# A six-block decoder: value projections moved into the router's gap, key rotation by a DVE shuffle, and a reordered start of attention

## The chip, the core and the metric

The kernel runs on one core of one Trainium2 chip. Its engines work side by side: PE multiplies matrices, DVE and POOL do elementwise work and reductions, ACT does functions and copies, SP only issues transfers. Every engine takes its own instructions in order and waits for the others through semaphores. The metric is the device time of one execution in microseconds, as the median of several runs.

## The reference, cut to what matters

A decoder of six blocks, each with a residual sum and a layer norm behind it. The input `x` is 4 sequences of 512 rows and 256 columns, the context 4 sequences of 1601 rows and 256 columns, all in float32.

```python
x = _layernorm(x + _L0_attn_ref(...))    # a recurrent layer (TTT)
x = _layernorm(x + _L0_xattn_ref(...))   # one-headed attention over the context
x = _layernorm(x + _L0_ffn_ref(...))     # 8 experts, the best 2 for each row
x = _layernorm(x + _L1_attn_ref(...))    # causal self-attention, 16 heads of 16
x = _layernorm(x + _L1_xattn_ref(...))   # cross-attention, 16 heads of 16, rotary
x = _layernorm(x + _L1_ffn_ref(...))     # dense feed-forward
```

The change concerns the third to the fifth block. In the fifth, queries and keys are projected, rotated and then used; the values are projected only:

```python
def apply_rope(x, cos, sin):
    x2 = jnp.stack([-x[..., 1::2], x[..., 0::2]], axis=-1).reshape(x.shape)
    return x * cos + x2 * sin
Q = (query @ Wq.T + bq)...; K = (key @ Wk.T + bk)...; V = (value @ Wv.T + bv)...
Q = apply_rope(Q, cos_q, sin_q); K = apply_rope(K, cos_k, sin_k)
```

`query` is `x`, `key` and `value` are the context. So keys and values of this block depend on nothing that the earlier blocks compute.

## The kernel before, in words

**Stages in time.** The recurrent layer runs to about 250 us, the one-headed attention and the router to 485 us, the experts from 521 to 1020 us, the fourth and fifth block from there to about 2335 us, and the last feed-forward behind them. Sequences (`b`), row tiles of 128 (`t`) and key tiles of 128 (`k`, 13 of them for the 1601 context rows, `NKT`) are the loop indices; the 16 heads form 4 groups (`g`, `NG`).

**Order of the work.** In most stages the program's own order is kept on every engine. What stands outside such a stretch (the loads of the attention weights into the pool `plw`, and `blocks_left`, which works out which expert blocks are left) is put in place by a planner that simulates a list schedule by readiness. Tiles of a pool that takes over the memory of an earlier pool wait until all of that pool's readers are through. `plw` and `p3` follow `p2in` and `p2` in this way.

**The router's gap (second block's end).** In pool `p2`, each step (b, t) makes scores, transposes the weights and sums the context rows with them (`weighted`). Behind the last `weighted` of a sequence follows the generator `closing(b)`: layer norm, `xT[b]` by transposes, then `route` (router logits, exponent, the best two, their ranks by a matmul) and `scatter(b)`, which writes the rows of `x` to the experts' list `xs` in DRAM by eight indirect transfers of POOL. `tail()` runs one step of such a generator. For the last sequence nothing else is left to do:

```python
        while tails:
            tail()
        ordered.close()
        scatter(B - 1, lambda inst: unordered("xs", inst))
```

Then the experts load their blocks of `xs` (`begin`, tile `xb`, L835) on SP, behind the loads of the attention weights (L79 to L85). The two biggest tiles of the stage's inputs are `fs`, the additive mask (128 x 4 x 1601), and `ctxa`, context rows of a sequence. Both are in `p2in` and read for the last time by the last scores and by the last `weighted`.

**The experts.** 23 blocks of 256 rows. `first_half` makes the gated hidden layer, `second_half` the second product, the norm, and `gamma` and `beta` on POOL (L909, L910); the result goes to `ys` in DRAM by an SP transfer. At each block one step of the generator `attention_first` runs, which prepares the next stage: context 0 into tiles (`qt`, `ks`), tables for the rotation, `vself`, `vals`, and at its end two small products for the output bias (`bo_x`, `bob`). It has 24 steps for 22 calls; what is left runs behind the last block.

**The gap behind the experts (L1010 on).** `combined(0)` gathers the experts' rows of sequence 0 by POOL's indirect transfers, adds them to `x` on DVE (`added`, L1091), normalizes, and transposes (`turned`). Only then can the self-attention of sequence 0 be projected: `self_rows(b, c)` makes key and query rows, which go through DRAM (`ksd`, `qd`) into the tiles of the head groups; `self_values(b)` makes its values. Meanwhile the kernel works on the contexts. `context(b, keys, values)` gives a list of small work items for a context: an item `key` (L1187) projects 512 keys of half the heads, evicts them by ACT into a `raw` tile (four buffers), rotates them and sends them to `kcd`; an item `value` (L1196) projects 128 rows by four matmuls of 256 columns and copies them by ACT into `vals[b % 2]`. Its context comes by SP transfers of 512 columns (`chunk`, two buffers). `rotated` (L1145 to L1157) makes the pair-swapped copy `swp` (two buffers) by two SP transfers between partitions of SBUF, then multiplies and adds on DVE for context 0 and on POOL for all others, queries included.

**The attention units.** 16 self units and then 16 cross units (b, g). A unit first takes maxima of its scores (`slot1`, DVE: L1272 in cross units, L1274 in self units), then for each key tile makes the scores again (L1315), exponents on ACT (L1329) and the weighted sums (L1342). Two lists carry other work into the units, one item at a time: `extras` (PE work: projections, keys and values of the next sequences) and `quiet`. `starts[i]` holds transfers that are issued as unit i begins. Keys and values of context 1 are made around the self units; those of contexts 2 and 3 in the cross units of sequences 0 to 2:

```python
        later = [
            context(2, range(4), ()) + context(3, range(2), ()),
            context(3, range(2, 4), ()) + context(2, (), range(4)),
            context(3, (), range(4)),
        ]
```

Of the kernel before, what the change touches and what calls it, by code (L numbers as in the profile page):

```python
# [9 lines left out]
F32 = mybir.dt.float32  # L10
# [3 lines left out]
ALU = mybir.AluOpType  # L14
# [20 lines left out]
def kn_of(kt):  # L35
    return P if kt < NKT - 1 else KLAST
# [3 lines left out]
def decoder(ctx: ExitStack, tc: tile.TileContext, a: dict, out: bass.AP):  # L40
    nc = tc.nc
# [16 lines left out]
    def bank():  # L58
        return psum["B"].tile([P, 512], F32, tag="bank", name="bank")
# [15 lines left out]
    def weight(pool, name):  # L75

        src = a[name]
        t = pool.tile([P, 2, src.shape[1]], F32, tag=name, name=name)
        nc.sync.dma_start(t, src.rearrange("(c p) n -> p c n", p=P))  # L79
        return t  # L80
# [117 lines left out]
    def mm(ps, terms):  # L198

        n = len(terms)  # L200
        for i, (l, r) in enumerate(terms):
            nc.tensor.matmul(ps, l, r, start=(i == 0), stop=(i == n - 1))  # L202
# [3 lines left out]
    p2in = ph2in.enter_context(tc.tile_pool(name="p2in", bufs=1))  # L206


    with (
# [15 lines left out]
        ps = wide()  # L225
# [4 lines left out]
        ps = bank()  # L230
# [7 lines left out]
        fs = p2in.tile([P, NT, S2], F32, tag="fs", name="fs")  # L238
# [7 lines left out]
        KHALF = (NKT + 1) // 2  # L246
# [358 lines left out]
        return wrow, xrow  # L605


    with tc.tile_pool(name="p2", bufs=2) as p2, ExitStack() as ordered:


# [131 lines left out]
        scored(*steps[0])  # L742
        tails = []

        def tail():
            if tails and next(tails[0], tails) is tails:
                tails.pop(0)

        for i in range(len(steps) + 1):
            if i + 1 < len(steps):  # L750
                b, t = steps[i + 1]
                scored(b, t)
                if t == NT - 1:
                    more_columns(b + 2)
                    if b + 1 < B:
                        queries(b + 1)
            tail()
            if i < len(steps):
                turned(*steps[i])
            tail()  # L760
            if i > 0:
                b, t = steps[i - 1]
                weighted(b, t)
                if t == NT - 1:
                    if b + 1 < B:
                        ctxns[b + 1] = load_ctx(b + 1)
                    tails.append(closing(b))
            tail()
        while tails:
            tail()  # L770
        ordered.close()
        scatter(B - 1, lambda inst: unordered("xs", inst))
        wrow, xrow = blocks_left()
# [5 lines left out]


    QS = 1.0 / math.sqrt(HD)
    VW = HD + 1
    p4a = late_a.enter_context(tc.tile_pool(name="p4a", bufs=1))
    mrow = tc.dram_tile((4 * B, S2), F32, name="mrow")
    live = p4a.tile([P, 4 * B], F32, tag="live", name="live")
# [35 lines left out]
    with tc.tile_pool(name="p3", bufs=2) as p3, ExitStack() as ordered:  # L821
# [70 lines left out]
        def second_half(i, wo, xb, g):  # L892
            ps = bank()
            pv = ps.rearrange("p (h d) -> p h d", d=D)
            for h in range(2):
                blk = slice(h * P, (h + 1) * P)
                mm(pv[:, h, :], [(g[:, f, blk], wo[:, f * D : (f + 1) * D]) for f in range(NF)])
            r = p3.tile([P, 2, D], F32, tag="rb", name="rb")
            nc.vector.tensor_tensor(r, pv, xb, ALU.add)  # L899
            mv = moments(r, 2)  # L900
            rs = rstd_of(mv, eps12, 2)
            for h in range(2):
                nc.vector.tensor_scalar(
                    r[:, h, :], r[:, h, :], mv[:, h, 0:1], rs[:, h : h + 1], ALU.subtract, ALU.mult
                )
            gam, bet = (
                wo[:, None, (NF + k) * D : (NF + k + 1) * D].to_broadcast([P, 2, D]) for k in (1, 2)
            )
            nc.gpsimd.tensor_tensor(r, r, gam, ALU.mult)  # L909
            nc.gpsimd.tensor_tensor(r, r, bet, ALU.add)  # L910
            nc.sync.dma_start(ys[i * BLK : (i + 1) * BLK, :].rearrange("(h p) d -> p h d", p=P), r)

        def attention_first():
# [5 lines left out]
            ready["later"] = p4a.tile([P, 2 * P], BF16, tag="later", name="later")  # L919
            yield  # L920
            nc.gpsimd.tensor_copy(ready["later"], later)
            yield
            qt, ks = ready["qt"], ready["ks"] = [group_tiles(p4a, n, S) for n in ("qt", "ks")]

            at = qt + ks
# [24 lines left out]
            for i in range(2 * NT):  # L950
                t = p4a.tile([P, 4, 32], F32, tag=f"ng{i}", name=f"ng{i}")
                nc.gpsimd.memset(t, 0.0)
                ngs.append(t)
            yield
            ready["vself"] = [values_tile(p4a, f"vs{i}", NT) for i in range(2)]
            yield
            ready["vals"] = [values_tile(p4a, "v0", NKT)]
            yield

# [68 lines left out]
    with ExitStack() as s4:  # L1028
# [107 lines left out]
        def self_values(b):  # L1136


            def item(k):
                ps = one()[:, :D]  # L1140
                mm(ps, [(xT[b][:, c, k * P : (k + 1) * P], W["qkvV"][:, c, :]) for c in range(2)])
                dst = vself[b % 2][:, k, : NH * VW].rearrange("p (h r) -> p h r", r=VW)
                nc.scalar.copy(dst[:, :, :HD], ps.rearrange("p (h r) -> p h r", r=HD))

            return [lambda k=k: item(k) for k in range(NT)]  # L1145

        def rotated(raw, n, ks, eng, tables=None):

            cos, sin = tables or (cosT[:, ks], sinT[:, ks])
            swp = p4.tile([P, S + 1], F32, tag="swp", name="swp")[:, :S]  # L1150
            pairs = raw.rearrange("(a two) n -> a two n", two=2)
            into = swp.rearrange("(a two) n -> a two n", two=2)
            for i in range(2):
                nc.sync.dma_start(into[:, i, :n], pairs[:, 1 - i, :n])
            eng.tensor_tensor(raw[:, :n], raw[:, :n], cos[:, :n], ALU.mult)  # L1155
            eng.tensor_tensor(swp[:, :n], swp[:, :n], sin[:, :n], ALU.mult)
            eng.tensor_tensor(raw[:, :n], raw[:, :n], swp[:, :n], ALU.add)  # L1157
# [3 lines left out]
        def flush(n):  # L1161
            while len(going) > n:
                going.pop(0)()
# [436 lines left out]
            f()  # L1600
        for f in first_sums:
            f()
        cosT = const(p4c, "c_cos", [P, S2], nc.sync)
        sinT = const(p4c, "c_sin", [P, S2], nc.sync)
        for f in context(0, (), range(4), here=qt + kself):
            f()

        keys0 = context(0, range(4), (), here=qt + kself)
        (k0_, q0_), rows0 = self_rows(0, 0)
        (k1_, q1_), rows1 = self_rows(0, 1)  # L1610
        for f in keys0[0:2] + keys0[4:6] + values1[:6] + add + values1[6:] + turn:
            f()
        for f in (k0_, q0_, rows0, *keys0[2:4], *keys0[6:8], *self_values(0), k1_, q1_, rows1):
            f()
        flush(0)
        for i, (n0, n1) in enumerate(((0, 4), (4, 6), (6, 7), (7, 8))):
            extras[i] = keys1[n0:n1] + extras[i]
        later = [
            context(2, range(4), ()) + context(3, range(2), ()),
            context(3, range(2, 4), ()) + context(2, (), range(4)),  # L1620
            context(3, (), range(4)),
        ]
        for b, work in enumerate(later):
            for g in range(NG):
                n = -(-len(work) // (NG - g))
# [233 lines left out]
```

## Time and profile before

| quantity | value |
|---|---|
| median of 3 runs | 2454.46 us (2454.04 to 2455.28) |
| the profiled execution | 2460.01 us, its span 2458.2 us |
| mean granted PE clock in it | 0.964 |
| PE busy | 2349.0 us (96%) |
| DVE busy | 1187.0 us (48%) |
| ACT busy | 1074.2 us (44%) |
| POOL busy | 425.0 us (17%) |

By stage, from the busy time of the engines in stretches of the span:

| stretch, us | PE busy | DVE | ACT | POOL | clock |
|---|---|---|---|---|---|
| 252 to 486, one-headed attention | 231.0 | 89.4 | 47.5 | 17.6 | 0.99 |
| 486 to 521, router's gap | 9.9 | 13.3 | 3.0 | 13.5 | 0.53 |
| 521 to 1020, experts | 494.1 | 135.5 | 236.4 | 161.0 | 0.99 |
| 1020 to 1148, gap and first maxima | 105.5 | 56.8 | 37.5 | 48.2 | 0.81 |
| 1148 to 1520, self units | 362.4 | 236.2 | 179.7 | 69.9 | 0.95 |
| 1520 to 2335, cross units | 814.5 | 527.6 | 499.8 | 86.5 | 1.00 |

How to read it: all times are of one profiled execution and are counted from its first instruction. "Busy" leaves out the issuing of transfers. The clock is the share of full speed that PE was granted in the stretch; at half the clock a matmul takes longer and still counts as busy. Where a row of an answer shows an instruction, it gives the start, the length, the engine, the line of the kernel, the operation, and the tiles that it writes and reads ("out<-in"); brackets hold the idle time of the engine before it and what ended it.

### The profile page before, as it was taken

The page shows a single profiled execution, that of the slowest core. Times are in us where ns is not written, and L with a number is a line of the kernel's source. Part 1 is how long each engine was busy: PE and PEld are TensorE (multiplying, and loading weights), DVE is VectorE, ACT ScalarE, POOL GpSimd, SP SyncE. Part 2 cuts the span into 40 slices and gives each one's busy share as a digit, 9 for nine tenths or more (in the row PEclk, how much of TensorE's full clock was granted, in tenths as well). Part 3 has the DMA queues.
Part 4 walks back from the last instruction along what each step waited for, and adds up shares of the span by engine and source line. Part 5 has one row for each costly group of instructions (what it writes and reads, how often), then busy time and mean ns, then how long its engine had stood idle before and what let it go on. Part 6 is the DMA issues. An engine that isn't in the chain of part 4 may idle for free.

```text
span 2458.2 us, 34942 instructions
## 1 busy us (share of the span) xinstructions
PE 2349.0 (96%) x13928; PEld 1331.3 (54%) x13928; DVE 1187.0 (48%) x2772; ACT 1074.2 (44%) x1996; POOL 425.0 (17%) x431
## 2 busy tenths in 40 slices
PE   7998999959999999969999999999999999999998
PEld 4767677748888888743333334333333333333256
DVE  1333334422222222336666667666666666677334
ACT  1111222114455544324555553655566565556730
POOL 1010001121134444323330000222110010000000
PEclk9999999969999999978999998999999999999999
DMA  8300211234767555442211220122210110110100
GB/s 319 135 1 23 102 54 44 73 135 149 263 251 273 212 190 197 145 122 81 83 44 30 71 75 5 49 73 62 66 54 20 44 40 16 32 36 16 33 9 26
DMA packets 82513, 224.50 MB, mean 91 GB/s; under 512 B 14120, under 2 KB 37934, under 8 KB 73262
## 3 DMA queue, kind: packets, MB, share of 16 engines
q1 hardware_dynamic: 68190, 141.70, 17.1%
q0 software_dynamic: 10992, 65.54, 7.3%
q10 hardware_dynamic: 3168, 15.03, 1.8%
q8 instruction: 110, 1.80, 0.3%
q14 instruction: 53, 0.43, 0.1%
HBM read 171.53 MB, written 53.21 MB: 91 GB/s over the span
## 4 chain that ended last, share of the span: by engine, by line
PE 51%; ACT 1%; DVE 1%; issue 0%; DVEq 0%; ACTq 0%
PE s L1315 23%; PE one L202 12%; PE po L1342 11%; PE s L202 2%; PE s L1325 1%; PE one L1300 1%; PE one L1363 1%; ACT x L171 0%; ACT ex L1329 0%; DVE one L1274 0%; PE one L1384 0%; PE one L1405 0%; PE one L1482 0%; DVE pm L1272 0%; DVE st L156 0%
## 5 line engine op out<-in xcount | busy, mean ns | idle before, releaser
L1329 ACT ACTIVATE ex<-s 128x512 f32<-128x512 f32 (+1 forms) x1062 | 578.1, 594 | 480.5 <-PE s L1315 237.4
L1272 DVE TENSOR_REDUCE pm<-one 128x1 f32<-128x512 f32 x768 | 494.2, 686 | 203.7 <-PE s L1315 147.7
L1315 PE MATMUL s<-q,kc 32*128 32x512 f32 x1612 | 522.9, 640 | 0.2 <-ACT ex L1329 0.2
L202 PE MATMUL one<-kc,qt 32*128 32x512 f32 (+1 forms) x2048 | 483.6, 563 | 0.3 <-DVE pm L1272 0.3
L1315 PEld LDWEIGHTS s<-q,kc 32*128 32x128 f32 x1612 | 161.6, 179 | 210.2 <-issue 175.2
L1342 PE MATMUL po<-ex,v 128*32 128x256 f32 (+3 forms) x2472 | 245.8, 466 | 0.3 <-ACT ot L1355 0.3
L1274 DVE CUSTOM_DVE_ANT_0 one<-one,c_diagq 128x512 f32<-128x512 f32 x256 | 172.0, 716 | 89.2 <-PE one L202 78.3
L1315 PE MATMUL s<-q,ks 32*128 32x512 f32 x512 | 182.2, 660 | 4.9 <-ACT ex L1329 4.9
L1342 PEld LDWEIGHTS po<-ex,v 128*32 128x32 f32 (+1 forms) x2472 | 49.9, 108 | 233.0 <-issue 227.0
L886 DVE TENSOR_TENSOR g<-g,sg 128x1024 f32<-128x1024 f32 x46 | 57.3, 1246 | 238.3 <-ACT sg L883 238.3
L202 PE MATMUL wide<-xbT,eWi 128*128 128x256 f32 x736 | 168.4, 388 | 4.0 <-DVE xbT L858 4.0
L202 PEld LDWEIGHTS one<-kc,qt 32*128 32x128 f32 x2048 | 163.9, 188 | 11.7 <-DVE pm L1272 7.7
L202 PE MATMUL bank<-eWo,g 128*128 128x256 f32 x736 | 162.8, 379 | 0.5 <-DVE rb L899 0.5
L202 PE MATMUL wide<-xbT,eWg 128*128 128x256 f32 x736 | 162.9, 379 | 0.1
L202 PEld LDWEIGHTS wide<-xbT,eWi 128*128 128x128 f32 x736 | 143.6, 195 | 25.1 <-issue 3.4
L1155 POOL TENSOR_TENSOR raw<-raw,c_cos 128x512 f32<-128x512 f32 (+1 forms) x32 | 35.0, 1093 | 696.2 <-DMA swp<-raw 616.5
L202 PE MATMUL one<-ks,qt 32*128 32x512 f32 x512 | 153.4, 668 | 1.1 <-ACT raw L1126 1.1
L202 PEld LDWEIGHTS wide<-xbT,eWg 128*128 128x128 f32 x736 | 139.8, 190 | 19.5 <-ACT g L883 0.5
L202 PEld LDWEIGHTS bank<-eWo,g 128*128 128x128 f32 x736 | 138.1, 190 | 18.5 <-DVE rb L899 0.6
L883 ACT ACTIVATE g<-wide,eWi 128x256 f32<-128x256 f32 x184 | 71.9, 477 | 69.8 <-PE wide L202 67.0
L1315 PEld LDWEIGHTS s<-q,ks 32*128 32x128 f32 x512 | 54.1, 188 | 83.1 <-issue 61.9
L202 PE MATMUL wide<-ctxT,q 128*128 128x512 f32 (+1 forms) x256 | 91.3, 510 | 0.8 <-DVE q L649 0.8
(310 smaller groups left out, 2969.7 us busy)
## 6 DMA issues: line engine op xcount, KB each, us to landing
xs<-zero SPq DMA_DIRECT2D x32, 512.0 KB
kc<-kcd SPq DMA_DIRECT2D x16, 800.5 KB
eWo<-in_eWo SPq DMA_DIRECT2D x8, 1408.0 KB
cx<-in_ctxT SPq DMA_DIRECT2D x18, 512.0 KB
eWi<-in_eWi SPq DMA_DIRECT2D x8, 1028.0 KB
eWg<-in_eWg SPq DMA_DIRECT2D x8, 1028.0 KB
swp<-raw SPq DMA_DIRECT2D x64, 128.0 KB
qt<-qd SPq DMA_DIRECT2D x32, 256.0 KB
```

The lines of the kernel that those rows point to most:

```text
L202: nc.tensor.matmul(ps, l, r, start=(i == 0), stop=(i == n - 1))
L883: nc.scalar.activation(dst[:, k, :], pv[:, k, :], func, bias=bias)
L886: nc.vector.tensor_tensor(part, part, dst, ALU.mult)
L1155: eng.tensor_tensor(raw[:, :n], raw[:, :n], cos[:, :n], ALU.mult)
L1272: nc.vector.tensor_reduce(pm[:, t, j, c : c + 1], ps, AX.X, ALU.max)
L1274: nc.vector.tensor_tensor_reduce(out=ps, in0=ps, in1=diagq[:, 384 - t * P : 896 - t * P], scale=1.0, scalar=LOWEST, op0=ALU.add, op1=ALU.m ...
L1300: nc.tensor.transpose(pt[:, t * P : (t + 1) * P], ng.rearrange("p j r -> p (j r)"), ident)
L1315: nc.tensor.matmul(ps[:kn], kt[rows, k * P : k * P + kn], q2[rows, :], start=True, stop=cross)
L1325: nc.tensor.matmul(ps[:, k * P : (k + 1) * P], later_[:, :P], later_[:, P:], start=False, stop=True)
L1329: nc.scalar.activation(ex[:kn, h, :], ps[:kn], AF.Exp)
L1342: nc.tensor.matmul(state["po"][j * 32 : j * 32 + 32, q0:q1], (vals if cross else vself)[b % 2][:kn, k, c0 : c0 + 32], ex[:kn, j % 2, q0:q1 ...
L1363: nc.tensor.transpose(pt[:, t * P : (t + 1) * P], ot[:, t * P : (t + 1) * P], ident)
```

## The change

1. **Values of contexts 2 and 3** (26 items of four matmuls and one ACT copy) are made in the `while tails` loop, two behind each `tail()`, and the rest behind it. They are written into new tiles in the places of `fs` and `ctxa`, whose fixed columns (zeros and ones) POOL writes by memsets, and stored to new DRAM tensors `vd[2]` and `vd[3]` by SP. One SP transfer for each loads `vals[b % 2]` as the second cross unit of the sequence before begins (`starts[index[b - 1, 1, True]]`). Their items go from `later`, and with them the context chunks loaded for them.
2. **The pair swap** in `rotated` is one `stream_shuffle` on DVE in place of two SP transfers, for all 40 rotations (8 of context 0, 24 of contexts 1 to 3, 8 of queries). The arithmetic stays where it was.
3. **`gamma` and `beta`** of the last expert block go to DVE.
4. **Three `yield`s** of `attention_first` are taken out, which leaves 21 steps.
5. **The order behind the experts**: all values of context 1 and the addition of the experts' rows come ahead of the second pair of keys; the values of the first self-attention come ahead of the other two pairs; the full cosine and sine tables are loaded behind this work instead of ahead of it; the second half of the first self-attention's projections (`k1_`, `q1_`, `rows1`) moves into the first unit's `extras`.

```diff
+        xaV = weight(p2, "xaV")
+        values, places = [], {}
+        def value(b, k):
+            if not places:
+                big = p2in.tile([P, NT * S2], F32, tag="fs", name="v23")
+                rest = p2in.tile([P, KHALF * D], F32, tag="ctxa", name="v2")
...
+                for b_ in (2, 3):
+                    nc.gpsimd.memset(places[b_, NKT - 1], 0.0)
...
+            kn = kn_of(k)
+            ps = bank()[:, :D]
+            mm(ps[:kn], [(ctxTs[b][:, c, k * P : k * P + kn], xaV[:, c, :]) for c in range(2)])
+            dst = places[b, k][:kn, : NH * VW].rearrange("p (h r) -> p h r", r=VW)
+            nc.scalar.copy(dst[:, :, :HD], ps[:kn].rearrange("p (h r) -> p h r", r=HD))
+            if b == 2 and k == NKT - 1:
+                nc.sync.dma_start(vd[2][:, : 9 * VROW], big_of(2, 0, 9))
+                nc.sync.dma_start(vd[2][:, 9 * VROW :], big_of(2, 9, NKT))
+            if b == 3 and k == NKT - 1:
+                nc.sync.dma_start(vd[3], big_of(3, 0, NKT))
...
+        values = [lambda b=b, k=k: value(b, k) for b in (2, 3) for k in range(NKT)]
         while tails:
             tail()
+            for f in values[:2]:
+                f()
+            values = values[2:]
+        for f in values:
+            f()
         ordered.close()
         scatter(B - 1, lambda inst: unordered("xs", inst))
...
-            nc.gpsimd.tensor_tensor(r, r, gam, ALU.mult)
-            nc.gpsimd.tensor_tensor(r, r, bet, ALU.add)
+            eng = nc.vector if i == E + NDYN - 1 else nc.gpsimd
+            eng.tensor_tensor(r, r, gam, ALU.mult)
+            eng.tensor_tensor(r, r, bet, ALU.add)
...
-            pairs = raw.rearrange("(a two) n -> a two n", two=2)
-            into = swp.rearrange("(a two) n -> a two n", two=2)
-            for i in range(2):
-                nc.sync.dma_start(into[:, i, :n], pairs[:, 1 - i, :n])
+            nc.vector.stream_shuffle(swp[:, :n], raw[:, :n], [i ^ 1 for i in range(32)])
...
-        cosT = const(p4c, "c_cos", [P, S2], nc.sync)
-        sinT = const(p4c, "c_sin", [P, S2], nc.sync)
...
-        for f in keys0[0:2] + keys0[4:6] + values1[:6] + add + values1[6:] + turn:
+        for f in keys0[0:2] + values1 + add + keys0[4:6] + turn:
             f()
-        for f in (k0_, q0_, rows0, *keys0[2:4], *keys0[6:8], *self_values(0), k1_, q1_, rows1):
+        for f in (k0_, q0_, rows0, *self_values(0), *keys0[2:4], *keys0[6:8]):
             f()
+        cosT = const(p4c, "c_cos", [P, S2], nc.sync)
+        sinT = const(p4c, "c_sin", [P, S2], nc.sync)
         flush(0)
...
-            extras[i] = keys1[n0:n1] + extras[i]
-        later = [
-            context(2, range(4), ()) + context(3, range(2), ()),
-            context(3, range(2, 4), ()) + context(2, (), range(4)),
-            context(3, (), range(4)),
-        ]
+            extras[i] = ([k1_, q1_, rows1] if i == 0 else []) + keys1[n0:n1] + extras[i]
+        later = [context(2, range(4), ()), context(3, range(4), ())]
+        for b in (2, 3):
+            starts[index[b - 1, 1, True]].append(
+                lambda b=b: nc.sync.dma_start(vals[b % 2].rearrange("p k r -> p (k r)"), vd[b])
+            )
```

More of the change, by code (lines that the diff above doesn't have):

```diff
@@ L605, in blocks_left @@
         return wrow, xrow
+    VW = HD + 1
+    VROW = NH * VW + HD - 1
+    vd = {b: tc.dram_tile((P, NKT * VROW), F32, name=f"vd{b}") for b in (2, 3)}
     with tc.tile_pool(name="p2", bufs=2) as p2, ExitStack() as ordered:
@@ L743, in decoder, with big_of @@
         tails = []
+        xaV = weight(p2, "xaV")
[4 more added lines that the diff above has]
+                rest = p2in.tile([P, KHALF * D], F32, tag="ctxa", name="v2")
+                for i in range(NKT):
+                    places[3, i] = big[:, i * VROW : (i + 1) * VROW]
+                    j = NKT + i
+                    places[2, i] = (
+                        big[:, j * VROW : (j + 1) * VROW] if i < 9 else rest[:, (i - 9) * VROW : (i - 8) * VROW]
+                    )
+                for b_ in (2, 3):
+                    nc.gpsimd.memset(places[b_, NKT - 1], 0.0)
+                for t in (big[:, : 22 * VROW], rest[:, : 4 * VROW]):
+                    t = t.rearrange("p (k r) -> p k r", r=VROW)
+                    nc.gpsimd.memset(t[:, :, NH * VW :], 0.0)
+                    heads = t[:, :, : NH * VW].rearrange("p k (h r) -> p k h r", r=VW)
+                    nc.gpsimd.memset(heads[:, :, :, HD : HD + 1], 1.0)
+            kn = kn_of(k)
[8 more added lines that the diff above has]
+                nc.sync.dma_start(vd[3], big_of(3, 0, NKT))
+        def big_of(b, k0, k1):
+            first = places[b, k0]
+            return bass.AP(first.tensor, first.offset, [first.ap[0], [1, (k1 - k0) * VROW]])
         def tail():
@@ L781, in decoder @@
     QS = 1.0 / math.sqrt(HD)
-    VW = HD + 1
     p4a = late_a.enter_context(tc.tile_pool(name="p4a", bufs=1))
@@ L921, in attention_first @@
             nc.gpsimd.tensor_copy(ready["later"], later)
-            yield
             qt, ks = ready["qt"], ready["ks"] = [group_tiles(p4a, n, S) for n in ("qt", "ks")]
@@ L953, in attention_first @@
                 ngs.append(t)
-            yield
             ready["vself"] = [values_tile(p4a, f"vs{i}", NT) for i in range(2)]
-            yield
             ready["vals"] = [values_tile(p4a, "v0", NKT)]
@@ L1610, in decoder @@
         (k1_, q1_), rows1 = self_rows(0, 1)
-        for f in keys0[0:2] + keys0[4:6] + values1[:6] + add + values1[6:] + turn:
+        for f in keys0[0:2] + values1 + add + keys0[4:6] + turn:
             f()
-        for f in (k0_, q0_, rows0, *keys0[2:4], *keys0[6:8], *self_values(0), k1_, q1_, rows1):
+        for f in (k0_, q0_, rows0, *self_values(0), *keys0[2:4], *keys0[6:8]):
             f()
+        cosT = const(p4c, "c_cos", [P, S2], nc.sync)
+        sinT = const(p4c, "c_sin", [P, S2], nc.sync)
         flush(0)
         for i, (n0, n1) in enumerate(((0, 4), (4, 6), (6, 7), (7, 8))):
-            extras[i] = keys1[n0:n1] + extras[i]
-        later = [
-            context(2, range(4), ()) + context(3, range(2), ()),
-            context(3, range(2, 4), ()) + context(2, (), range(4)),
-            context(3, (), range(4)),
-        ]
+            extras[i] = ([k1_, q1_, rows1] if i == 0 else []) + keys1[n0:n1] + extras[i]
[3 more added lines that the diff above has]
+                lambda b=b: nc.sync.dma_start(vals[b % 2].rearrange("p k r -> p (k r)"), vd[b])
+            )
         for b, work in enumerate(later):
```

## The prediction

> **What bounds the kernel now.** I read the chain of work that ended last first, then the windows by stage, then single engines' timelines where PE has holes. The chain can be followed back to 1162 us of the 2458.2, and nearly all of that is PE:
>
> ```profile
> PE 51%; ACT 1%; DVE 1%; issue 0%; DVEq 0%; ACTq 0%
> ```
>
> So work taken off PE behind 1162 us should show in the time. How much of it does? ACT's timeline in a cross-attention unit answers (start, length, instruction; the brackets hold idle time before it):
>
> ```profile
> 1844.37 1.09 ACT L1329 ACTIVATE ex<-s 128x512 f32<-128x512 f32 x2 [0.51 <-PE one L202]
> 1846.35 1.08 ACT L1329 ACTIVATE ex<-s 128x512 f32<-128x512 f32 x2 [0.89 <-PE s L1315]
> 1847.93 1.08 ACT L1329 ACTIVATE ex<-s 128x512 f32<-128x512 f32 x2 [0.50 <-PE one L202]
> 1850.26 1.09 ACT L1329 ACTIVATE ex<-s 128x512 f32<-128x512 f32 x2 [1.25 <-PE s L1315]
> 1851.28 0.38 ACT L1196 COPY v<-one 128x256 f32<-128x256 f32 x1
> 1852.33 1.09 ACT L1329 ACTIVATE ex<-s 128x512 f32<-128x512 f32 x2 [0.68 <-PE s L1315]
> ```
>
> Two pairs of exponents make one key tile. Without other work it takes 1847.93 - 1844.37 = 3.56 us, with one value item (L1196) 1852.33 - 1847.93 = 4.40. Over all such tiles of the cross stage the medians are 3.49 us (77 tiles) and 4.27 (24): 0.78 us per value item, a little under its four matmuls (4 x 0.214 = 0.86).
>
> The windows (PE, PEld, DVE, ACT, POOL busy, clock, DMA) show two holes, the router's gap and the gap behind the experts:
>
> ```profile
> 485.00:521.00 36.00, 10.28 (x40) 8.60 (x38) 13.87 (x76) 3.03 (x5) 13.48 (x14) 0.54 0.38 124
> 1020.00:1076.00 56.00, 40.33 (x136) 28.23 (x134) 18.38 (x39) 16.40 (x39) 33.16 (x36) 0.79 0.42 136
> 1076.00:1102.00 26.00, 19.18 (x56) 9.91 (x56) 5.43 (x13) 6.24 (x14) 0.00 (x0) 0.87 0.47 137
> ```
>
> In the second hole DVE's timeline tells what is late:
>
> ```profile
> 1047.78 0.69 DVE L1155 TENSOR_TENSOR raw<-raw,xT 128x512 f32<-128x512 f32 x1 [22.45 <-DMA swp<-raw]
> ...
> 1059.50 1.09 DVE L1091 SCALAR_TENSOR_TENSOR x<-ex,ws,x 128x256 f32<-128x256 f32 x2
> ...
> 1091.99 0.69 DVE L1155 TENSOR_TENSOR raw<-raw,xT 128x512 f32<-128x512 f32 x1 [24.84 <-DMA swp<-raw]
> ...
> 1101.64 0.69 DVE L1274 CUSTOM_DVE_ANT_0 one<-one,c_diagq 128x512 f32<-128x512 f32 x1
> ```
>
> The experts' rows were issued to be gathered from 1029.23 to 1039.1, but their addition (L1091) stands in DVE's queue behind four rotations that wait for swap DMAs, to 1059.50. Later four more such waits hold the first attention maximum until 1101.64.
>
> The first hole, by SP's and POOL's queues:
>
> ```profile
> 485.39 0.37 SPq L79 DMA_DIRECT2D qkvQ<-in_qkvQ  x1
> ...
> 492.60 0.25 SPq L85 DMA_DIRECT2D xa_bo<-in_xa_bo  x1
> 518.52 0.89 SPq L835 DMA_DIRECT2D xb<-xs  x2
> ```
> ```profile
> 504.83 0.96 POOL L534 DMA_INDIRECT xs<-x,rows  x1 [1.95 <-DMA xs<-x,rows]
> 507.09 0.96 POOL L534 DMA_INDIRECT xs<-x,rows  x1 [1.30 <-DVE cum L562]
> ...
> 515.97 0.96 POOL L534 DMA_INDIRECT xs<-x,rows  x1 [0.30 <-issue]
> ```
>
> The row numbers of the last sequence end at 506.8, eight scatters follow, and the experts' first load goes at 518.52. PE waits through it.
>
> **The skill.** "TensorE: Matmul & The Clock Gate", Part 1: an idle window halves PE's clock, and engines other than PE take instructions in strict order. The trace agrees: 0.54 granted in the router's gap; DVE's addition above waits for its turn. "VectorE: DVE Perf Modes", perf-mode tier table: a shuffle runs only at 1x, some 2400 ns for 2048 elements, near the fp32 tensor_tensor's 2293. The trace has no shuffle, but its tensor_tensor of 512 takes 0.69 us, which I take for it (bounds 0.6 and 0.9). "DMA: Bandwidth & Descriptors", Anatomy of one DMA: about 2 us fixed; here the last `ys` store held POOL 2.40 us.
>
> **1. Values leave the cross stage.** 26 items x 0.78 = -20.2 us (bounds -16, if tiles hit ACT's pace, and -22.3, all matmuls). Their eight context loads go too; two loads of `vd`, 1.91 MB each (128 x 3731 x 4 B), come on SP three units before use: at the 299 GB/s that the first 50 us moved some 6.4 us each, under PE. DMA is 13% busy there: 0.
>
> **2. The gap behind the experts.** (a) gamma and beta on DVE: 2 x 0.69 for POOL's 2 x 1.26: -1.2 us on the way to the `ys` store. (b) Three yields fewer let the `bob` matmuls, done from 1020.2 to 1024.9, run under the experts; values of context 0 start near 1021 instead of 1025.5, and warm. They are 11.2 us (13 x 0.86), to 1032.4; two keys (4 x 0.43 each) to 1035.9. (c) DVE rotates these: 4 x about 0.68 = 2.7 each, to 1040.3; then the addition, which took 6.9 us, to 1047.3. (d) ACT cannot take the root before its copies of context 1's values. PE makes them from 1035.9, but the third chunk is loaded only when the first is free (1039.3) and takes 5.3 us as at 1054.35: the copies end at 1049.7. Root 0.9, application 2.1, two key evictions 1.4, transposes' copies 1.1: the first K projection at 1055.4 instead of 1076.2. (e) From there the rows' round trip stays: 4.1 us from `ksd` store to its load, 2.5 us more for its neighbours; a `raw` tile (four buffers) comes free behind it, near 1070.4. Four rotations, two of them 65 wide, need 2 x 2.7 + 2 x 0.9: DVE is free for the maxima at 1078 instead of 1101.6. Sum of the gap: -23 us (bounds -14, if SP's chunk and row transfers queue up, and -27). Second-half projections (4 x 2 x 0.43) move into unit 0's maximum phase, where DVE sets the pace and PE has room: 0, or +3.4 if not. The cosine tables, moved behind on SP, are wanted only at POOL's first rotation.
>
> **3. Rotation on DVE elsewhere.** 32 shuffles (24 keys, 8 queries), 0.69 each = 22 us, in DVE's strict order ahead of the maxima. A key tile takes 5.11 us, and DVE's four maxima 2.7, so the shuffle fits; a wait on ACT's eviction can still push the maxima 0.35 us. I take +3 in all (bounds 0 and +10). Cover gone, it is 22. 64 of the 80 swap DMAs go here, hidden already (POOL's 616 us of waiting cost nothing).
>
> **4. The router's gap.** New: 26 x 4 matmuls, 22.3 us of PE, 26 ACT copies x 0.37, seven POOL memsets (nearest rows 0.27 and 0.45 for 195 and 208 elements: about 2.3 us), three stores. Each step of the last `closing` has two items behind it, so transposes, router product and rank product queue behind two to four items, and two banks tie the items to ACT. I count +0.8 at the transposes, +1.3 before the exponent, +1 at the ranks: +3; the warm clock (24 router matmuls took 6 us here, 3.4 before) is in it. POOL's memsets fall behind the third sequence's scatters (505.8) and before the last's. The last item ends near 515, its store needs 6.4 + 2.4: 524. Now SP: the weights' loads, 7.5 us of issue, wait until the old pool is read out, so for that store. If the planner leaves them ahead of `xb`, that goes at 532, +13; if it puts `xb` first, it follows the store on the same rings, +5. I take +9 (bounds +3, +16).
>
> Sum: -20.2 - 23 + 3 + 9 = -31 us. The profiled execution, 2460.0 with a span of 2458.2, becomes 2429; it ran 5.5 above the median of the runs, 2454.5, which becomes 2423.
>
> **Rivals.** *The gap's gain is eaten:* stores hold SP, the experts start 16 us late, and the second gap gives 14: -20.2 - 14 + 3 + 16 = -15, 2439. For it: 485 to 492 shows the weights first; against: `xb` can go first. *Values are hidden anyway:* were cross tiles bound by ACT, step 1 gives 8 instead of 20: 2435. Against: 3.49 and 4.27. *Slower:* shuffles in DVE's queue wait for ACT and for `swp` (two buffers; a POOL rotation takes 3 x 1.27 = 3.8 us); PE follows. Without them the sum is -34; from 1.1 us of PE per shuffle it is lost, at 2 us (64) the time is 2484. Against: key tiles come 5 us apart. *The shuffle doesn't replace the DMAs* cannot be: they are gone from the code.
>
> **Numbers.** Forecast 0.62; first rival 0.15, second 0.11; slower one 0.08; 0.04 that losses just cancel. The 8 in 10 reach from 2404 (step 1 at -22.3, step 2 at -27, step 3 at 0, step 4 at +3 less about 4 for a warm start of the experts, whose first half took 9.96 us where 7.07 is usual, which leaves -50) to 2443 (-16 - 14 + 3 + 16 = -11), which takes in the first two rivals. Faster by over 0.2% (4.9 us, what a measurement here can tell) 0.88, within 0.04, slower 0.08.
>
> **What would show it.** Cross tiles all near 3.5 or 5.1; first L1091 near 1040 and first L1274 near 1078, counted from the experts' end; `xb` 5 or 13 us later; a shuffle of 0.7. Wrong if DVE's maxima wait behind shuffles, or the experts start over 20 us late.

## The result

The changed kernel takes 2439.88 us (median of 5 runs, 2437.56 to 2441.9), the kernel before 2454.46: a ratio of 0.9932, 95% interval 0.9918 to 0.9945. That is 14.6 us faster. 31 were forecast (2423, range 2404 to 2443), so the direction and the range held and the forecast was about twice too large.

The two profiled executions differ by more than the medians: the spans are 2458.2 and 2438.1, a difference of 20.1 us. The one of before ran 5.5 us above its median, the one after (2439.88) at its median. The differences by stretch below add up to the 20.1. "Experts' start" is their first product of weights (L202 `wide<-xbT,eWi`), their end the last product with `eWo`; a unit ends with ACT's `ot` copy.

| stretch | before | after | difference | forecast |
|---|---|---|---|---|
| to the last weighted matmul of the second block | 485.36 | 488.62 | +3.26 | 0 |
| from there to the experts' start | 37.87 | 56.85 | +18.98 | +9 |
| the experts | 497.04 | 495.25 | -1.79 | 0 |
| experts' end to the first attention maximum | 81.37 | 54.55 | -26.82 | -23 |
| first maximum to the end of unit 0 | 46.93 | 51.65 | +4.72 | 0 to +3.4 |
| units 1 to 15 | 360.87 | 356.57 | -4.30 | in the +3 |
| units 16 to 31 (cross) | 825.52 | 811.21 | -14.31 | -20.2 + 3 |
| the rest | 123.26 | 123.40 | +0.14 | 0 |

So the router's gap lost twice what was forecast, and that is where most of the expected gain went. Some lines carry chance: kernels of the experiments below with the same program up to the last weighted matmul (e3, e5, e6, e7) reach its end at 482.1 to 487.7 us, so the +3.26 is not shown to come from the change. With the same program behind the experts (e1, e2, e4, e8), the first maximum comes 50.4 to 54.4 us behind the experts' end, and from it unit 0 takes 48.6 to 52.1. The router's gap itself is steady: 56.9 to 58.8 us in the changed kernel, e3, e5, e6 and e7, which have the same program there.

Line numbers of the changed kernel are some 40 to 46 higher in the later stages: L1091 is L1135 now, L1274 is L1315.

The chain that ended last is as before nearly all PE:

```profile
PE 50%; DVE 1%; ACT 1%; issue 0%; DVEq 0%; ACTq 0%
```

A cross unit of sequence 2 (unit 26), which had value items before, by ACT's timeline:

```profile
2040.75 1.08 ACT L1370 ACTIVATE ex<-s 128x512 f32<-128x512 f32 x2 [0.82 <-PE s L1356]
2042.33 1.08 ACT L1370 ACTIVATE ex<-s 128x512 f32<-128x512 f32 x2 [0.49 <-PE one L202]
2044.24 1.09 ACT L1370 ACTIVATE ex<-s 128x512 f32<-128x512 f32 x2 [0.82 <-PE s L1356]
```

Its tiles are 3.49 us apart now; no tile with a value item is left.

The windows of the two holes (length; PE, PEld, DVE, ACT, POOL busy; clock; DMA share; GB/s):

```profile
488.00:546.00 58.00, 34.05 (x150) 28.62 (x149) 14.70 (x75) 12.41 (x31) 15.31 (x20) 0.75 0.25 96
1040.00:1076.00 36.00, 32.00 (x133) 23.66 (x132) 16.81 (x41) 16.68 (x40) 21.55 (x24) 1.00 0.44 137
1076.00:1096.00 20.00, 14.86 (x48) 8.07 (x46) 13.14 (x31) 4.78 (x11) 11.17 (x10) 0.85 0.58 167
```

The hole behind the experts has closed in its first part: 32.0 us of 36 busy at full clock, where it was 40.3 of 56 at 0.79. Its second part, up to the first maximum, still has 14.9 of 20. The router's hole has grown from 36 us to 58.

DVE's timeline behind the experts, which end at 1040.72:

```profile
1055.65 0.72 DVE L1195 STREAM_SHUFFLE swp<-raw 128x512 f32<-128x512 f32 x1
...
1061.04 1.00 DVE L1135 SCALAR_TENSOR_TENSOR x<-ex,ws,x 128x256 f32<-128x256 f32 x2
...
1094.46 0.23 DVE L1195 STREAM_SHUFFLE swp<-raw 128x65 f32<-128x65 f32 x1
...
1095.27 0.69 DVE L1315 CUSTOM_DVE_ANT_0 one<-one,c_diagq 128x512 f32<-128x512 f32 x1
```

The addition starts 20.3 us behind the experts' end (39.2 before), the first maximum 54.6 behind it. A shuffle of 512 takes 0.72 us.

Now the router's gap, engine by engine: PE, ACT, POOL, and SP's queue.

```profile
488.45 1.89 PE L202 MATMUL bank<-xaV,ctxT 128*128 128x256 f32 x8
504.79 3.78 PE L202 MATMUL bank<-xaV,ctxT 128*128 128x256 f32 x8 [14.44 <-ACT v L775]
508.36 1.70 PE L188 MATMUL wide<-ident,x 128*128 128x128 f32 x8
```

```profile
491.09 0.20 ACT L127 ACTIVATE rstd<-sd 128x4 f32<-128x4 f32 x1
504.36 0.65 ACT L775 COPY v<-bank 128x256 f32<-128x256 f32 x2 [13.06 <-POOL v L770]
```

```profile
501.55 0.96 POOL L534 DMA_INDIRECT xs<-x,rows  x1 [1.70 <-DMA xs<-x,rows]
502.51 0.62 POOL L765 MEMSET v<- 128x287 f32 x2
...
504.29 0.21 POOL L770 MEMSET v<- 128x64 f32 x1
529.23 0.96 POOL L534 DMA_INDIRECT xs<-x,rows  x1 [24.74 <-DVE rows L521]
```

```profile
523.36 0.34 SPq L778 DMA_DIRECT2D vd<-v  x1
540.57 0.37 SPq L881 DMA_DIRECT2D xb<-xs  x1
541.00 0.46 SPq L780 DMA_DIRECT2D vd<-v  x1
...
549.67 0.38 SPq L79 DMA_DIRECT2D qkvQ<-in_qkvQ  x1
```

PE makes two value items and then stands for 14.4 us: both banks are full, and ACT's first copy (L775) waits for POOL's memsets of the same tile. Those stand in POOL's queue behind the eight scatters of the third sequence, which go one at a time, 2.66 us each. The transposes of the last sequence (L188), on which the whole rest of the routing hangs, stand behind the two waiting items in PE's order. Stores, memory pools and weights have next to no part in it: the first load of `xb` goes at 540.57, as soon as SP's wait for the scatters' landing is over (540.54), 2.5 us behind the start of the last scatter, as before the change (515.97 and 518.52). It goes ahead of the third store and of the weights' loads. The third store stands between it and the second load of `xb`, and takes some 0.5 us of SP there.

### The profile page after: what moved, and what is told of

It is laid out like the page before. It is cut to its first block, busy times and chain, and to the rows that moved or that the text cites. A ratio compares the mean times of both kernels' runs of the same rounds, so it can differ in the third digit from the quotient of the medians.

```text
span 2438.1 us, 35300 instructions
## 1 busy us (share of the span) xinstructions
PE 2344.9 (96%) x14144; PEld 1335.7 (55%) x14144; DVE 1212.4 (50%) x2854; ACT 1074.8 (44%) x1996; POOL 426.0 (17%) x435
## 3 DMA queue, kind: packets, MB, share of 16 engines
q1 hardware_dynamic: 60606, 137.66, 16.4%
## 4 chain that ended last, share of the span: by engine, by line
PE 50%; DVE 1%; ACT 1%; issue 0%; DVEq 0%; ACTq 0%
PE s L1356 22%; PE po L1383 11%; PE one L202 11%; PE s L202 2%; PE s L1366 1%; PE one L1341 1%; PE one L1404 1%; ACT x L171 0%; ACT ex L1370 0%; DVE pm L1313 0%; DVE one L1315 0%; PE one L1425 0%; PE one L1523 0%; PE one L1446 0%; DVE nb L166 0%
## 5 line engine op out<-in xcount | busy, mean ns | idle before, releaser
L1356 PE MATMUL s<-q,kc 32*128 32x512 f32 x1612 | 529.9, 640 | 0.8 <-ACT ex L1370 0.8
L202 PE MATMUL one<-kc,qt 32*128 32x512 f32 (+1 forms) x2048 | 484.5, 564 | 0.3 <-DVE pm L1313 0.3
L1383 PE MATMUL po<-ex,v 128*32 128x256 f32 (+3 forms) x2688 | 252.2, 444 | 0.3 <-ACT ot L1396 0.3
L1315 DVE CUSTOM_DVE_ANT_0 one<-one,c_diagq 128x512 f32<-128x512 f32 x256 | 171.9, 716 | 75.1 <-PE one L202 63.0
L202 PEld LDWEIGHTS one<-kc,qt 32*128 32x128 f32 x2048 | 164.6, 189 | 11.9 <-DVE pm L1313 8.3
L202 PE MATMUL wide<-xbT,eWi 128*128 128x256 f32 x736 | 165.6, 384 | 4.0 <-DVE xbT L904 4.0
L202 PE MATMUL wide<-xbT,eWg 128*128 128x256 f32 x736 | 162.9, 379 | 0.0
L202 PE MATMUL bank<-eWo,g 128*128 128x256 f32 x736 | 162.5, 379 | 0.0
L202 PE MATMUL one<-ks,qt 32*128 32x512 f32 x512 | 152.1, 661 | 5.1 <-ACT raw L1228 4.0
L202 PEld LDWEIGHTS wide<-xbT,eWi 128*128 128x128 f32 x736 | 141.2, 192 | 24.8 <-issue 4.2
L202 PEld LDWEIGHTS wide<-xbT,eWg 128*128 128x128 f32 x736 | 139.8, 190 | 19.4 <-ACT g L929 0.5
L202 PEld LDWEIGHTS bank<-eWo,g 128*128 128x128 f32 x736 | 138.2, 190 | 17.9
L1196 POOL TENSOR_TENSOR raw<-raw,c_cos 128x512 f32<-128x512 f32 (+1 forms) x32 | 34.9, 1092 | 637.2 <-DVE swp L1195 613.9
L202 PE MATMUL wide<-ctxT,q 128*128 128x512 f32 (+1 forms) x256 | 91.3, 510 | 0.8 <-DVE q L654 0.8
```

Source lines behind the costliest of these rows:

```text
L1315: nc.vector.tensor_tensor_reduce(out=ps, in0=ps, in1=diagq[:, 384 - t * P : 896 - t * P], scale=1.0, scalar=LOWEST, op0=ALU.add, op1=ALU.m ...
L1356: nc.tensor.matmul(ps[:kn], kt[rows, k * P : k * P + kn], q2[rows, :], start=True, stop=cross)
L1383: nc.tensor.matmul(state["po"][j * 32 : j * 32 + 32, q0:q1], (vals if cross else vself)[b % 2][:kn, k, c0 : c0 + 32], ex[:kn, j % 2, q0:q1 ...
```

## The experiments

Ratios are to the kernel before, with its 95% interval; the kernels ran in three groups (e1 to e4; e5, e6, e8, e9; e7, e10), each beside its own runs of the kernel before, so the ratios compare better than the medians.

| kernel | median, us | ratio | profiled span, us |
|---|---|---|---|
| changed kernel | 2439.88 | 0.9932 (0.9918 to 0.9945) | 2438.1 |
| e1: memsets on DVE | 2427.07 | 0.9906 (0.9891 to 0.9922) | 2423.1 |
| e2: e1, items placed by step | 2418.03 | 0.9876 (0.9857 to 0.9895) | 2413.9 |
| e4: values back in the cross units | 2435.91 | 0.9936 (0.9922 to 0.9951) | 2435.8 |
| e3: swap by SP transfers | 2441.73 | 0.9955 (0.9937 to 0.9972) | 2440.8 |
| e5: second half back in the gap | 2438.50 | 0.9929 (0.9907 to 0.9952) | 2441.3 |
| e6: old order, with the shuffle | 2449.77 | 0.9971 (0.9960 to 0.9982) | 2449.6 |
| e7: yields, gamma and beta back | 2440.68 | 0.9931 (0.9916 to 0.9946) | 2432.3 |
| e8: e2, memsets early | 2417.46 | 0.9852 (0.9818 to 0.9885) | 2413.8 |
| e9: e8, shuffle for context 0 alone | 2411.24 | 0.9822 (0.9791 to 0.9853) | 2404.6 |
| e10: e8, queries' swap by transfers | 2414.84 | 0.9834 (0.9803 to 0.9864) | 2411.1 |

### The wait for the memsets (e1, e2, e8)

Theory M: the memsets behind the scatters. Rivals: the prediction's own reason (S, stores and weights in SP's queue) and PE's order of items (F).

```diff
-                    nc.gpsimd.memset(...)      # the three places of value()
+                    nc.vector.memset(...)
```

> The changed kernel with one edit: the seven memsets of the fixed columns for the moved values are DVE's, not POOL's. Theory M: what the router's gap lost (56.9 us from the last weighted matmul to the experts' first product, 37.9 before) is mostly ACT's first value copy, which waits for POOL's memsets behind eight chained scatters (PE idle from 490.3 to 504.8). Then that stretch falls to 42 to 45 us and the time by 12 to 15 us, to about 2426. Theory S (the prediction's step 4: stores and weights on SP hold the experts' first load): nothing changes, 2440. Theory F (PE's order: items in front of the router's steps): at most 2 us.

PE's timeline of it:

```profile
484.85 1.89 PE L202 MATMUL bank<-xaV,ctxT 128*128 128x256 f32 x8
491.43 3.46 PE L202 MATMUL bank<-xaV,ctxT 128*128 128x256 f32 x8 [4.68 <-ACT v L775]
...
529.56 5.92 PE L202 MATMUL wide<-xbT,eWi 128*128 128x256 f32 x13 [0.78 <-DVE xbT L904]
```

From the last weighted matmul (485.02) to the experts' start it takes 44.5 us instead of 56.9: 12.3 less by this edit alone, as M had it. S, which expected no change, falls. The wait that is left, 4.7 us, is for DVE's memsets (489.12 to 491.07), which stand behind the last norm in its queue.

```diff
+        fills = [2, 2, 1, 0, 0, 2, 2, 2]
         while tails:
             tail()
-            for f in values[:2]:
+            n = fills.pop(0) if fills else 0
+            for f in values[:n]:
                 f()
-            values = values[2:]
+            values = values[n:]
```

> As e1_memsets_dve, and the number of value items behind each step of the last closing is 2, 2, 1, 0, 0, 2, 2, 2 and then all that is left behind the rank product, so that none stands between the transposes' copy and the router product, or ahead of the exponent. Theory M with F as its rest: the stretch falls by 3 to 6 us more, to about 38 to 40, and the time to about 2421. If M alone is at work: as e1.

The stretch is 40.6 us, 4.0 less again, so F holds for its part. In the changed kernel the router product stood behind four items, and ACT's exponent behind two copies of items that PE had not made yet; here PE does the router product 0.2 us after its input is there:

```profile
495.45 1.03 PE L202 MATMUL bank<-xaV,ctxT 128*128 128x256 f32 x4
496.72 0.61 PE L202 MATMUL bank<-Wr,xT 128*128 128x8 f32 x4 [0.23 <-ACT xT L196]
...
507.74 13.22 PE L202 MATMUL bank<-xaV,ctxT 128*128 128x256 f32 x60
```

Fifteen items (60 matmuls) run behind the rank product while POOL scatters, where hardly anything waits for them: SP's wait for PE ahead of the first load of `xb` is 0.5 us.

```diff
+            if i == len(steps) - 1:
+                big_ready()        # POOL's memsets, ahead of scatter(2)
 ...
+            rest_ready()           # DVE's, behind the last norm
```

> As e2_memsets_dve_fill, but the memsets of the tile in the place of the mask are POOL's and stand ahead of the third sequence's scatters, where the mask has been read; those of the four items in the place of the context rows are DVE's, behind the last norm. e2 has 4.7 us of idle PE left (486.6 to 491.3), where ACT's first copy waits for DVE's memsets. If that wait is on the path, the experts start 3 to 5 us sooner and the time is 2413 to 2415; if PE then waits for the norm instead (its first item is ready 6 us ahead of the transposes), 2416 to 2418.

PE's second pair of items waits 1.3 us now:

```profile
485.41 1.99 PE L202 MATMUL bank<-xaV,ctxT 128*128 128x256 f32 x8 [1.27 <-ACT v L759]
```

The stretch falls to 39.1 us, within 1.3 us of the kernel before, with 22 us more of PE's work in it. What is left is no longer the memsets: the scatters have landed by 514.8, and SP waits 1.8 us more for PE, until its last value item is through (516.47), before the first load of `xb` goes (516.50). e9 and e10, with the same program there, show 1.7 and 1.6 us of this wait. So the room behind the rank product is not quite large enough for these items. The span is the same as e2's (2413.8 and 2413.9), in part because the gap behind the experts was longer: from the experts' end to the first K projection 36.0 us against 32.4 in e2. The program is the same there, so the edit did not do this. It goes with the group of runs: e1, e2 and e4, of one group, have 32.4 to 32.8 us, and the changed kernel, e8 and e10, of others, 34.9 to 36.0. e8 is not shown to be faster than e2.

### Values back in the cross units (e4)

```diff
-        values = [lambda b=b, k=k: value(b, k) for b in (2, 3) for k in range(NKT)]
 ...
-        later = [context(2, range(4), ()), context(3, range(4), ())]
+        later = [
+            context(2, range(4), ()) + context(3, range(2), ()),
+            context(3, range(2, 4), ()) + context(2, (), range(4)),
+            context(3, (), range(4)),
+        ]
```

> The changed kernel with its first part undone: values of contexts 2 and 3 in the cross units again, in the old three lists. By the profile of the changed kernel the router's gap then gives back 19 us (and 3 us ahead of it that may be chance) and the cross units take 14 to 17 more: 2433 to 2438. By the prediction's terms (20.2 gained, 9 and 3 lost) it would be slower than the changed kernel by 8 to 11 us: 2448 to 2451.

2435.91, as the profile of the changed kernel had it and not as the prediction had it. The experts' start is back at 37.9 us behind the last weighted matmul, and the cross units take 824.9 us (811.2 in the changed kernel). Its ratio, 0.9936, is that of the changed kernel, 0.9932: the first part of the change, as it was made, gave nothing that these runs can tell. Without the wait and with the items placed (e2, 0.9876) it is worth 0.6%, by intervals that don't touch.

### Shuffle and order behind the experts (e3, e6)

```diff
-            nc.vector.stream_shuffle(swp[:, :n], raw[:, :n], [i ^ 1 for i in range(32)])
+            for i in range(2):
+                nc.sync.dma_start(into[:, i, :n], pairs[:, 1 - i, :n])
```

> The changed kernel with the pair swap by two SP transfers again, all else as changed. Prediction's view: the shuffle costs some 3 us in the units and what the gap gains needs it, since DVE's rotations wait for swaps ahead of the experts' addition and of the maxima: the gap is 10 to 20 us longer, units 1 to 3 us shorter, 2447 to 2459. View that the order alone gives the gain: 2437 to 2440. View that shuffles in DVE's queue cost PE 0.3 us or more each in the units (32 of them): 2430.

2441.73, lower than the prediction's view and higher than each of the two others; its interval overlaps that of the changed kernel. From the experts' end (1041.21) to the first maximum it takes 64.0 us, 9.4 more than in the changed kernel and 12.4 to 13.6 more than in e1, e2 and e4 of its own group. The waits for swaps are back, but shorter than the 22 to 25 us of before:

```profile
1063.24 0.69 DVE L1199 TENSOR_TENSOR raw<-raw,xT 128x512 f32<-128x512 f32 x1 [1.18 <-DMA swp<-raw]
...
1065.26 1.34 DVE L1135 SCALAR_TENSOR_TENSOR x<-ex,ws,x 128x256 f32<-128x256 f32 x2
...
1078.13 0.69 DVE L1199 TENSOR_TENSOR raw<-raw,xT 128x512 f32<-128x512 f32 x1 [5.42 <-DMA swp<-raw]
...
1095.07 0.98 DVE L1199 TENSOR_TENSOR raw<-raw,xT 128x512 f32<-128x512 f32 x1 [8.18 <-DMA swp<-raw]
```

Behind unit 0 it is 4.3 us shorter than the changed kernel, and its cross units took 805.8 us: 19.7 less than before, with the values moved and no shuffles in them.

```diff
-        for f in keys0[0:2] + values1 + add + keys0[4:6] + turn:
+        for f in keys0[0:2] + keys0[4:6] + values1[:6] + add + values1[6:] + turn:
 ...
-        for f in (k0_, q0_, rows0, *self_values(0), *keys0[2:4], *keys0[6:8]):
+        for f in (k0_, q0_, rows0, *keys0[2:4], *keys0[6:8], *self_values(0), k1_, q1_, rows1):
```

> The changed kernel with the old order behind the experts (the second pair of keys ahead of the addition, the tables' loads ahead of the keys, values and second half last), the shuffle kept. With e3_swap_dma, which keeps the order and drops the shuffle, this parts the gain of 26.8 us from the experts' end to the first maximum: e3 keeps 17.4 of it. If the two parts only add up, this kernel keeps about 9 us and the maximum comes 17 us later than in the changed kernel (about 72 us behind the experts' end; 2450 to 2457). If either alone does most of it, since each takes away the same wait, it keeps 17 or more (under 64 us; 2440 to 2448).

The first maximum comes 66.9 us behind the experts' end. So of the 26.8 us, the order (with parts 3 and 4) keeps 17.4 without the shuffle, and the shuffle keeps 14.5 without the order. The two sum to 5.1 us more than the whole, but with the spread of 50.4 to 54.6 us for kernels that have both, what they share lies anywhere between 1 and 5 us. Neither expectation was met; the result lies between. With the old order the addition stands behind four rotations again (26.1 us behind the experts' end), now of 2.7 us each. The maximum waits for PE, whose products stood 5.6 us behind an eviction of ACT; that waited 6.4 us for a `raw` tile, until its rows were stored to DRAM (`kcd`):

```profile
1067.54 1.21 DVE L1135 SCALAR_TENSOR_TENSOR x<-ex,ws,x 128x256 f32<-128x256 f32 x2
...
1108.29 0.70 DVE L1315 CUSTOM_DVE_ANT_0 one<-one,c_diagq 128x512 f32<-128x512 f32 x1 [6.90 <-PE one L202]
```

### The small parts (e5, e7)

```diff
-            extras[i] = ([k1_, q1_, rows1] if i == 0 else []) + keys1[n0:n1] + extras[i]
+            extras[i] = keys1[n0:n1] + extras[i]      # k1_, q1_, rows1 behind keys0[6:8]
```

> The changed kernel with the second half of the first self-attention's projections back in the gap, behind the other keys. In the changed kernel the stretch from the first maximum to the first exponent takes 26.3 us, and 22.7 before. The prediction gave this part 0 to 3.4 us of loss in unit 0. If that move is what lengthened the stretch, it falls by 3 to 4 us here, and the first maximum comes 0 to 6 us later: between 2437 and 2443. If it lengthened for another reason (keys of context 1, swaps), the stretch stays at 26 and the time rises by 2 to 6.

No difference in time that can be told (the interval is 0.2% to each side). The first maximum comes 55.5 us behind the experts' end, against 54.6, and the stretch to the first exponent is 26.1 us, against 26.3. The four projections are gone from that stretch, but it had a clock of 0.63, where the changed kernel had 0.76. e8, of the same group and with the projections in the stretch, has 23.9 us at 0.86. Length times clock is 20.0 to 20.5 us with the projections there (changed kernel, e1, e2, e8) and 15.9 to 16.8 without (before, e5, e6). So, by estimate, the projections cost some 4 us of full clock in the stretch, about the 3.4 that the prediction allowed for, and the clock decides what of it shows. What set the clock in each execution stays open.

```diff
-            eng = nc.vector if i == E + NDYN - 1 else nc.gpsimd
+            eng = nc.gpsimd
 ...
+            yield      # in the three places
```

> The changed kernel with its third and fourth part undone: gamma and beta of the last block on POOL and the three yields back. By the prediction's steps 2a and 2b the experts' last rows reach DRAM 1.2 us later, and the first value of context 1's neighbour, context 0, starts 4.5 us later behind the experts' end: the addition starts 4 to 6 us later (25 us behind the experts' end, 20.3 in the changed kernel) and the time is 2443 to 2446. Rival: the addition waits for the gathered rows or the first rotation alone, and the output-bias matmuls go into a hole anyway: 0 to 2 us, 2440 to 2442.

The addition starts 25.8 us behind the experts' end, 5.5 later than in the changed kernel, as steps 2a and 2b have it. But the first maximum comes only 2.2 us later (56.7 against 54.6, and 54.5 in e10 of its own group), and the ratios are equal (0.9931 and 0.9932). These two parts did what was forecast to the addition; at the maximum 2.2 us of it are left, and in the time none that can be told.

### Shuffles in the units (e9, e10)

```diff
+            if tables:      # context 0
+                nc.vector.stream_shuffle(swp[:, :n], raw[:, :n], [i ^ 1 for i in range(32)])
+            else:           # the two transfers of before
```

> As e8_memsets_early, with the shuffle only for context 0, and the two SP transfers again for the 24 other keys and the 8 queries, all of which POOL rotates. In e3_swap_dma the units whose second tile holds a query's rotation (21, 25, 29) took 1.35, 0.64 and 3.19 us less than with the shuffle. View Q (a query's or key's shuffle holds DVE's queue until ACT's eviction): 4 to 6 us less than e8. View that e3's gain is chance: the same as e8.

2411.24, ratio 0.9822: the lowest median of this study, 1.8% under the kernel before, and under the changed kernel by intervals that don't touch. Against e8 the intervals overlap, and most of what differs in the two profiles is not the shuffle itself. Units 28 and 29, together 3.2 us shorter here than in the changed kernel, hold no rotation at all: the last shuffle of the changed kernel stands in unit 27, so the two expectations above and below that count unit 29 among those with a query's rotation are wrong in this. In the changed kernel the end of unit 28 and the start of unit 29 ran at half clock with PE recorded as busy all the time. The two windows, first 7 us of the unit in the changed kernel, and the same 7 us in e9:

```profile
2187.00:2194.00 7.00, 7.00 (x36) 1.79 (x32) 2.96 (x10) 2.92 (x7) 0.00 (x0) 0.61 0.00 1
```

```profile
2156.65:2163.65 7.00, 7.00 (x52) 2.39 (x52) 5.77 (x16) 5.42 (x12) 0.00 (x0) 1.00 0.00 0
```

36 matmuls against 52 in the same time. Against e8, units 4, 8 and 9 are 1.5 to 1.6 us shorter in e9 and units 13 and 15 as much longer, steps that also come between kernels with the same program there (last section). What is left for the shuffles is 1.3 us in unit 21 and 0.3 in unit 25 (queries), and at most 2.7 in unit 0's tiles.

```diff
-                rotated(raw, S, slice(0, S), nc.gpsimd)
+                rotated(raw, S, slice(0, S), nc.gpsimd, shuffled=False)      # queries alone
```

> As e8_memsets_early, with the two SP transfers again for the 8 queries only; all keys keep the shuffle. e9_early_swap_units differs from e8 in unit 0 (2.7 us), unit 21 (1.3), unit 25 (0.3) and unit 29 (3.2, there by a stretch at half the PE clock). Units 21, 25 and 29 hold query rotations, unit 0 keys. If the shuffles of queries cost time, units 21 and 25 are as in e9 (53.8 and 51.4 us between ends), unit 0 as in e8; time 2412 to 2416. If those of keys do: all as in e8 but for chance, 2416 to 2419.

2414.84, between e8 and e9, with overlapping intervals. Unit 25 is as in e9 (51.1), unit 21 nearer to e8 (54.8, where e8 has 55.1 and e9 53.8). Units 28 and 29 have no half clock here, with the keys' shuffles in place. Which shuffles cost the little that they cost is not settled.

## Why the prediction was right, and where it was too large

**Step 4, the router's gap, is the step that failed.** It forecast +9 (bounds +3 and +16) and measured +19, beyond its bounds. The place was right and the mechanism wrong. It let `xb` wait on SP for the last store and for the weights; in the trace `xb` went ahead of both, and e1, which leaves SP's queue as it is, took 12.3 us away. The step did see that "POOL's memsets fall behind the third sequence's scatters (505.8)", and priced them as 2.3 us of POOL's time (it counted seven; the trace has six, 2.1 us). What it left out is who waits for them: ACT's first copy, so both banks, so PE, and in PE's order the transposes of the last sequence. Its +3 for items ahead of the router's steps was the right kind of term and near the right size: e2 took 4.0 us away. In the profile the experts start 22.2 us later (545.47 against 523.23), 19.0 of them from this gap, so one of the prediction's own signs of being wrong ("over 20 us late") came true.

**Step 1 was right in size.** It said -20.2 us for 26 value items. With no shuffles in the cross units (e3) they took 19.7 us less than before, in e9 19.4. Of this, 1.6 us is a stretch at half clock in units 28 and 29 that the kernel before has and these two have not, so some 18 us are left for the values, between the bounds of 16 and 22.3. The changed kernel gained 14.3; step 3 has the difference.

**Step 3** took +3 for shuffles in the units. The cross units of the changed kernel take 5.4 us more than those of e3, of which 3.2 are the stretch at half clock in units 28 and 29. A stretch like it is in the changed kernel, e1, e2 (there half as long), e5, e6 and e8, but not in e4 or e7, which have the same shuffles. The kernel before, which has none, has it too, half as long. So shuffles are not needed for it; whether they make it longer stays open. Of the shuffle's duration, 0.69 was taken and 0.72 measured. The slower rival needed 1.1 us of PE for each; the 5.4 us are 0.25 for each of the 22 shuffles in the cross units, and 0.1 without the stretch.

**Step 2, the gap behind the experts, was right almost throughout**, counted from the experts' end: addition at 20.3 us (20.1 forecast), first K projection at 34.9 (35.2), first maximum at 54.6 (57.8). Unit 0 gave 4.7 us back, where 0 to 3.4 was allowed for. Counted to the end of unit 0 the gap gained 22.1, and 23 was said. That the two meet so closely is in part luck: in e1, e2, e4 and e8, with the same program there, the end of unit 0 comes 100.2 to 103.5 us behind the experts' end, in the changed kernel 106.2. The parts within it are less sure than the sum: e7 has the 5.5 us of parts 3 and 4 at the addition worth about 2 at the maximum, and e3 and e6 have the order and the shuffle share some of their gain.

**The conversion to the median** was off too. The prediction carried the 5.5 us by which the profiled execution of before ran above the median into both kernels. The profile of the changed kernel ran at its median. Of the 16.4 us between forecast and measurement (31 and 14.6), the profiles explain 10.9 (20.1 against 31) and this the rest, 5.5.

**The rivals.** The first one named 2439, which is what came, from a late start of the experts and a smaller gain in the second gap. The first half of it came true in effect (the experts ended 20.5 us later), by another cause; the second half did not. The range held with 3 us to spare, and its upper end had been built from this rival's terms, so that the measurement fell within it owes something to luck: the forecast's own reason for the loss was not the one at work.

## What to carry to other kernels

Work put into an idle stretch brings its preparation along: look up in which queue each memset, load or store of it lands, what stands ahead of it there, and who waits for it. Here six memsets of 2.1 us in all, in the wrong engine's queue, took back 12.3 of the roughly 18 us that 26 moved items gained. And filler that stands in an engine's order ahead of a step on the chain holds up that step: here taking it away from in front of the router product and of the exponent, and putting 15 of the 26 items behind the rank product, where POOL's scatters leave room, gave 4.0 us. That room has an end as well: with the items placed so and the memsets early (e8), the last of them hold up the next load by 1.8 us.

## What was not expected of the hardware

PE's granted clock falls to half at places where PE is recorded as busy without a break. "TensorE: Matmul & The Clock Gate" of the Trainium skill, Part 1, explains half clock by an idle window. Before the change, 1484 to 1512, in the maxima of the first cross unit:

```profile
1484.00:1512.00 28.00, 28.00 (x113) 16.54 (x116) 20.86 (x36) 3.06 (x6) 0.00 (x0) 0.57 0.00 1
```

28.0 us of 28.0 busy, at 0.57. No idle window is recorded here, neither in the stretch nor in the 3.4 us ahead of it (busy 3.41 of 3.41), so the trace does not agree with that account as it stands. But the recorded ends of matmuls are modelled, and in those 3.4 us PE has 13 matmuls, where the four such windows from 1464.2 to 1477.8 have 30 to 36 each; PE may have been less loaded than its record says. Most matmuls of the stretch read 32 rows each; whether that is the reason was not tested. Single stretches of 3.41 us at half clock come at other places in other executions: unit 4 took 24.5 us in the profiles of the changed kernel, e2 and e4 and 26.0 in those of e1 and e8, which have the same program there. In e1 PE was busy for 1.73 of the 3.41 us ahead of that stretch (1204.40), so this stretch is nearer to the page's account. A difference of 1.5 us in one unit between two profiles therefore says nothing by itself, and spans can differ by several.
